# Weighted sums first, scores between them, row sums of four together: the dense attention steps of the later images

## The chip, the core and the metric

The kernel runs on one core of a Trainium2 chip. The metric is the device time of one execution in microseconds. Below, TensorE is the matrix engine (PE in the profile), VectorE is DVE, ScalarE is ACT, GpSimd is POOL, and SyncE (SP) issues most of the transfers.

## The reference

Two layers run one after the other on 8 images of 512 channels and 32 x 32 = 1024 tokens. Layer 0 is a group norm, attention with 8 heads whose q, k and v are rounded to 8 bits, a projection and a residual. Layer 1 is a group norm, attention with one head over all 512 channels, a projection and a residual. Cut to what matters here:

```python
# layer 0, x is (8, 512, 32, 32), T = 1024, 8 heads of 64 channels
h = group_norm(xf, gn_w, gn_b)
q, k, v = split(qkv_w @ h + qkv_b)          # each through fake_quant (8 bits)
w = softmax((q * scale)^T (k * scale))      # per head, T x T
a = einsum('bts,bcs->bct', w, v)            # weighted sums over the keys
x = xf + proj_w @ a + proj_b
# layer 1 on the result: one head of 512 channels
x = x + wp @ (softmax(q1 k1^T / sqrt(512)) v1) + bp
```

## The kernel before

**The phases.** First all images' q, k and v of layer 0 are computed and kept in DRAM, since the rounding needs the extremes over all images. Then layer 0's attention runs through all images as one stream, and layer 0's projection and the whole of layer 1 of an image run beside the attention of the images after it. The attention is a generator, `attention()`; the projection and layer 1 are another, `others()`. At each yield of `others()` the loop at the end (L1898 to L1900) lets the attention go one step further, and so attention steps come between the blocks of projection and layer 1 on TensorE, in the order written.

**Units.** A unit is one block of 128 keys, for a pair of heads and 512 queries: 8 images x 4 pairs x 2 halves x 8 blocks = 512 units. A step of the generator handles four of them, u to u+3. For a unit:

- `scores(u)` (L1009) makes the products of k and q: four matmuls for two units, "st<-q,k" in the profile, 64 rows for each head. They go to a tile of `pair_ps`, from the pool `ps_s`, which has two buffers; one tile takes two banks. ScalarE takes the exponential of the tile ("pt<-st,esc", L1034) and so frees it.
- `split(u)` (L1040) makes the f16 pair: the exponential cast to f16 (by ScalarE, or by GpSimd for every fourth unit) and the remainder, which VectorE computes ("two<-pt,two").
- `over_keys(us)` (L1090) makes the weighted sums, "av<-two,v": eight matmuls a unit, on 32 columns each.
- `totals(us)` (L1115) makes the row sums of the exponentials, "sm<-two,ones": four matmuls a unit, on 32 columns each.

A step works on weighted sums and row sums of u to u+3, on scores of u+6 to u+9, and on splits of u+6 to u+9.

**Three kinds of steps.** `dense` and `late` are set from what `others()` yields (L1899). A plain step (yield 1) takes the weighted sums and the row sums of four units together. A dense step (yield -1) takes two and two. A late step (yield 2) comes after the second half of the projection. Dense steps come just before a projection and between its two halves, `first()` at L1724 and `project` at L1292; image 0 has them at other places (the first step under the planner, between the halves of its projection, and in `layer1` at L1623).

**The projection.** `project` (L1260) makes, for each half, four output blocks of four matmuls over the channels ("pj<-ao,wp", two records each in the profile, 128 columns of 512). VectorE adds bias and residual to each block ("h<-pj,vec,h", L1278), which frees its bank. For image 0 the banks come from `ps_o`. For the later images `first()` passes `score_bank`, so the blocks take turns with the scores in the two buffers of `ps_s`:

```python
def score_bank(name):
    return pair_ps(name)[:, 0, :]
...
yield -1
yield from project(b + 1, score_bank)
yield 2
```

**What sets the order.** Every engine's instructions are recorded in program order and kept in it (`InOrder`, and `mm` at L208 for TensorE). Once `InOrder.planned` is set (L1893), small works of VectorE and ScalarE are held in lists with a cost and a due time, and are put into the stream by a model of the time: `pe.t` counts TensorE's, `do` and `fill` (L104, L127) place the works that fit before the next fixed one, and `awaits` moves `pe.t` for what a matmul waits for. The model's `scores` waits for the exponential that frees its tile; the projection's matmuls don't count that wait.

The function that the diff touches, and what calls it:

Of the kernel before, what the change touches and what calls it, by code (L numbers as in the profile page):

```python
# [58 lines left out]
def attn_pair_kernel(  # L59
# [12 lines left out]
    class InOrder:  # L72
# [74 lines left out]
        def settle(self, what):  # L147

            while True:
                i = next((i for i, c in enumerate(self.chores) if c[0] == what), None)  # L150
                if i is None:
                    return
                self.begin(i)
# [10 lines left out]
    def awaits(t):  # L164

        pe.t = max(pe.t, t + 0.1)
# [41 lines left out]
    def mm(ps, lhsT, rhs, **kw):  # L208
        ins = nc.tensor.matmul(ps, lhsT=lhsT, rhs=rhs, **kw).ins  # L209
        part = lhsT.shape[-1] / P if lhsT.shape[-1] in (32, 64) else 1.0  # L210
        if rhs.dtype in (BF, F16, F32R):
            part *= 0.25 * lhsT.shape[0] / P
        pe.t += math.prod(rhs.shape[1:]) * 1.677e-3 * part
        if last_mm[0] is not None:
            tc.add_manual_dep(ins, last_mm[0].name, IN_ORDER, reason="order")
        last_mm[0] = ins
# [90 lines left out]
    with ExitStack() as fast:  # L307
# [4 lines left out]
        def av_bank(name):  # L312
            return ps_v.tile([P, 512], F32, tag="v", name=name)
# [78 lines left out]
        with tc.tile_pool(name="p1w", bufs=1) as p1w, tc.tile_pool(  # L392
# [3 lines left out]
            def one(name):  # L396
                return ps_1.tile([P, 512], F32, tag="b", name=name)
# [313 lines left out]
            late = [one(f"qkps_0_{PAIRS}_{hf}") for hf in range(NH)]  # L711
# [201 lines left out]
        def plain(b, s):  # L913
            return b == 0 and s % 4 == 3
# [80 lines left out]
        def attention():  # L995
# [86 lines left out]
            def need(u):  # L1082

                if u in put_off:
                    put_off.pop(u)()
                while u not in ready:
                    e, name = (act, "cast") if u not in at_hand else (dve, "sum")
                    e.begin(next(i for i, c in enumerate(e.chores) if c[0] == name))

            def over_keys(us):  # L1090
                need(us[-1])
                awaits(ready[us[-1]])
                pe.t += 0.12
                for u in us:
                    b, j, hf, s = units[u]
                    if s == 0:
                        avs[b, j, hf] = av_bank(f"av_{b}_{j}_{hf}")
                    if plain(b, s):
                        for i in range(4):
                            r = slice(i * QUAD, (i + 1) * QUAD)  # L1100
                            mm(
                                avs[b, j, hf][r, :], lhsT=vfs[j][:, s // 4, r],
                                rhs=parts[u][:, i // 2, :], start=False, stop=(s == NT - 1),
                            )
                        continue
                    for w in range(2):
                        for i in range(4):
                            r = slice(i * QUAD, (i + 1) * QUAD)
                            mm(
                                avs[b, j, hf][r, :], lhsT=pairs[b, j][2][:, s, r],  # L1110
                                rhs=parts[u][:, w, i // 2, :], start=(s == 0 and w == 0),
                                stop=(s == NT - 1 and w == 1),
                            )

            def totals(us):  # L1115
                pe.t += 0.12
                for u in us:
                    b, j, hf, s = units[u]
                    if s == 0:
                        sms[b, j, hf] = av_bank(f"sm_{b}_{j}_{hf}")  # L1120
                    if plain(b, s) and s < NT - 1:
                        continue
                    for n in range(4):
                        row = sms[b, j, hf][n * QUAD : (n + 1) * QUAD, :]
                        if plain(b, s):
                            mm(row, lhsT=ones[:, 0:QUAD], rhs=parts[u - 4 + n // 2 * 4][:, n % 2, :],
                               start=False, stop=True)
                        else:
                            mm(row, lhsT=ones16, rhs=parts[u][:, n // 2, n % 2, :], start=(s == 0),
                               stop=(s == NT - 1))  # L1130
                    for v in (u - 4, u) if plain(b, s) else (u,):
                        del parts[v]
# [56 lines left out]
            for u in range(0, len(units), 4):  # L1189
                b, j, hf, s = units[u]  # L1190
                if hf == 0 and s == 0:
                    n = b * PAIRS + j + 1
                    if n < B * PAIRS:
                        pairs[divmod(n, PAIRS)] = load_pair(*divmod(n, PAIRS), u)
                    settle("qv")

                def two(what, v):  # L1200
                    if v < len(units):
                        what(v)
                        what(v + 1)

                pe.t += 0.12
                if not late:
                    two(scores, u + 6)
                if late:
                    over_keys((u, u + 1))
                    two(scores, u + 6)  # L1210
                    totals((u, u + 1))
                    over_keys((u + 2, u + 3))
                    totals((u + 2, u + 3))
                    two(split, u + 6)
                    two(scores, u + 8)
                elif dense:
                    over_keys((u, u + 1))
                    totals((u, u + 1))
                    two(split, u + 6)
                    two(scores, u + 8)  # L1220
                    over_keys((u + 2, u + 3))
                    totals((u + 2, u + 3))
                else:
                    over_keys(range(u, u + 4))
                    totals(range(u, u + 4))
                    two(split, u + 6)
                    two(scores, u + 8)
                if s == NT - 4:
                    finish(b, j, hf, u)
                two(split, u + 8)  # L1230
                pe.t += 0.15
                last = (j, hf, s) == (PAIRS - 1, NH - 1, NT - 4)
                yield b + last
# [616 lines left out]


        att = attention()
        done = 0
        dense = True
        late = False
# [42 lines left out]
        for n in others():  # L1898
            dense, late = n < 0, n == 2  # L1899
# [365 lines left out]
```

## Time and profile before

| what | value |
|---|---|
| time, median of 3 runs | 2581.56 us (2579.74 to 2581.93) |
| the profiled execution, its own time | 2581.92 us |
| its span | 2580.1 us |
| TensorE matmul busy | 2525.0 us, 98% of the span |
| VectorE busy | 1897.2 us, 74% |
| ScalarE busy | 1346.8 us, 52% |
| granted TensorE clock, mean | 0.995 |

The profile is one execution. A line of the profile's timeline has start, length, engine, source line, operation, what is written and read, shape, count, and in brackets the idle time ahead of it with what ended it. The matmuls' ends are modelled and overlap with the next, so the length of a block of matmuls is read from its start to the next block's. Since all engines' operations are recorded by helpers (L91, L209), operations are told apart by the tiles that they write and read.

### The profile page before, as it was taken

How to read it: one execution, taken by the hardware profiler on the slowest of the kernel's cores; microseconds unless marked ns; L12 is line 12 of the kernel's file. 1: busy time of each engine (PE TensorE's matmuls, PEld its weight loads, DVE VectorE, ACT ScalarE, POOL GpSimd, SP SyncE). 2: the span in 40 equal slices, each digit the busy share in tenths (PEclk: the TensorE clock that was granted, in tenths of full speed). 3: DMA queues.
4: the chain of work that ended last, by engine and by line, in shares of the span. 5: the costliest groups of instructions: out<-in, count | busy, mean ns of one | idle time of the engine just before them, and what ended most of it. 6: DMA issues, size and time to landing. Idle time of an engine off the chain costs nothing.

```text
span 2580.1 us, 38716 instructions
## 1 busy us (share of the span) xinstructions
PE 2525.0 (98%) x15670; PEld 1751.9 (68%) x15670; DVE 1897.2 (74%) x2747; ACT 1346.8 (52%) x1684; POOL 185.3 (7%) x167
## 2 busy tenths in 40 slices
PE   7999999998999999999999999999999999999998
PEld 4788888872247766775777577657756775777787
DVE  6788777667978777776777787777778777775544
ACT  3222222217947665665666466747665665664121
POOL 0000000001110001000100010010001000100000
PEclk9999999999999999999999999999999999999999
DMA  4343333336621232123213321332232123212211
GB/s 168 134 147 138 113 120 120 131 123 180 148 88 63 87 103 100 50 79 119 87 55 103 100 87 58 100 114 67 71 115 91 49 76 123 88 49 83 86 38 39
DMA packets 160189, 250.69 MB, mean 97 GB/s; under 512 B 27008, under 2 KB 93568, under 8 KB 158464
## 3 DMA queue, kind: packets, MB, share of 16 engines
q1 hardware_dynamic: 125264, 182.81, 21.3%
q10 hardware_dynamic: 30560, 57.71, 6.5%
q0 software_dynamic: 4176, 7.60, 1.6%
q8 instruction: 125, 2.05, 0.3%
q14 instruction: 64, 0.52, 0.1%
HBM read 153.64 MB, written 86.28 MB: 93 GB/s over the span
## 4 chain that ended last, share of the span: by engine, by line
PE 85%; DVE 5%; issue 2%; ACT 2%; DMA 1%; POOL 0%; SPq 0%; ACTq 0%; DVEq 0%; POOLq 0%
PE s L209 15%; PE o L209 13%; PE qkps L209 12%; PE pj L209 9%; PE av L209 8%; PE v2ps L209 7%; PE vps L209 6%; PE g L209 6%; PE st L209 4%; PE sm L209 3%; DVE two L91 2%; ACT pt L91 1%; DVE h L91 1%; PE fold L209 1%; DMA two<-spare 1%
## 5 line engine op out<-in xcount | busy, mean ns | idle before, releaser
L91 ACT ACTIVATE pt<-st,esc 128x1024 f32<-128x1024 f32 x467 | 496.4, 1114 | 333.8 <-PE st L209 316.3
L91 DVE TENSOR_TENSOR two<-pt,two 128x1024 f16<-128x1024 f32 x467 | 561.9, 1217 | 136.8 <-POOL two L1069 101.9
L91 ACT CAST two<-pt 128x1024 f16<-128x1024 f32 x346 | 350.7, 1055 | 7.7 <-ACT p L91 5.1
L209 PE MATMUL av<-two,v 128*32 128x512 f16 x3968 | 248.4, 383 | 8.2 <-DVE two L91 5.6
L1069 POOL CAST two<-pt 128x1024 f16<-128x1024 f32 x112 | 145.4, 1298 | 1412.2 <-ACT pt L91 714.8
L209 PE MATMUL s<-g,h 128*128 128x256 f32 x1024 | 233.4, 381 | 0.0
L209 PE MATMUL pj<-ao,wp 128*128 128x512 f32 x512 | 223.6, 595 | 0.0
L209 PEld LDWEIGHTS s<-g,h 128*128 128x128 f32 x1024 | 193.1, 190 | 30.8 <-issue 4.3
L91 ACT ACTIVATE u_ring<-qkps,qkbt 128x512 f32<-128x512 f32 x89 | 61.0, 685 | 252.5 <-PE qkps L209 235.7
L209 PEld LDWEIGHTS <-v 128*32 128x32 f16 x3968 | 92.3, 96 | 147.7 <-issue 75.2
L209 PE MATMUL s<-g,sums 128*128 128x256 f32 x768 | 178.5, 381 | 0.2 <-DVE p L91 0.2
L209 PEld LDWEIGHTS pj<-ao,wp 128*128 128x128 f32 x512 | 96.2, 190 | 121.2 <-issue 111.6
L209 PE MATMUL st<-q,k 64*128 64x512 bf16 x1024 | 164.4, 384 | 12.7 <-ACT pt L91 7.1
L209 PE MATMUL o<-p,v 128*128 128x256 f32 x768 | 175.2, 382 | 1.0 <-DVE p L91 1.0
L209 PEld LDWEIGHTS o<-p,v 128*128 128x128 f32 x768 | 144.4, 190 | 26.9 <-issue 5.7
L209 PEld LDWEIGHTS s<-g,sums 128*128 128x128 f32 x768 | 144.8, 190 | 24.3 <-issue 4.6
L209 PE MATMUL sm<-two,ones 128*32 128x512 f16 x1984 | 137.4, 382 | 0.0
L209 PE MATMUL qkps<-half,w_high 128*128 128x512 f32 x480 | 134.4, 403 | 0.0
L209 PE MATMUL qkps<-half,w_low 128*128 128x512 f32 x480 | 131.8, 397 | 2.3 <-DVE half L91 2.3
L209 PEld LDWEIGHTS <-k 64*128 64x128 bf16 x1024 | 35.0, 94 | 144.9 <-issue 142.8
L209 PE MATMUL qkps<-half,w_mix 128*128 128x512 f32 x480 | 131.2, 396 | 1.1 <-DVE half L91 1.1
L209 PE MATMUL v2ps<-wm,h 128*128 128x256 f32 x512 | 119.9, 384 | 1.9 <-ACT g L91 1.3
(225 smaller groups left out, 3906.5 us busy)
## 6 DMA issues: line engine op xcount, KB each, us to landing
rs<-rs_d SPq DMA_DIRECT2D x76, 256.0 KB
x<-in_x_dram SPq DMA_DIRECT2D x32, 512.0 KB
q_d<-wa SPq DMA_DIRECT2D x32, 512.0 KB
k_d<-wa SPq DMA_DIRECT2D x32, 512.0 KB
v_d<-v_ring SPq DMA_DIRECT2D x32, 512.0 KB
raw<-q_d SPq DMA_DIRECT2D x32, 512.0 KB
raw<-k_d SPq DMA_DIRECT2D x32, 512.0 KB
x_d<-h SPq DMA_DIRECT2D x64, 256.0 KB
```

Of the source, the lines that this page charges most:

```text
L91: ins = self.latest = op(*args, **kw).ins
L209: ins = nc.tensor.matmul(ps, lhsT=lhsT, rhs=rhs, **kw).ins
L1069: copy(two[:, 0], pt)
```

## The change

In dense steps under the planner, the scores of u+6 and u+7 no longer open the step: the weighted sums of u and u+1 do, then come those scores, then the weighted sums of u+2 and u+3, then the row sums of all four units, and the scores of u+8 and u+9 end the step. The dense steps of the first image's attention, which run before the planner is on, keep their order, as do plain and late steps.

```diff
                 pe.t += 0.12
-                if not late:
+                if not late and not (dense and InOrder.planned):
                     two(scores, u + 6)
                 if late:
                     over_keys((u, u + 1))
...
                     two(split, u + 6)
                     two(scores, u + 8)
+                elif dense and InOrder.planned:
+                    over_keys((u, u + 1))
+                    two(scores, u + 6)
+                    over_keys((u + 2, u + 3))
+                    totals(range(u, u + 4))
+                    two(split, u + 6)
+                    two(scores, u + 8)
                 elif dense:
                     over_keys((u, u + 1))
                     totals((u, u + 1))
                     two(split, u + 6)
                     two(scores, u + 8)
                     over_keys((u + 2, u + 3))
                     totals((u + 2, u + 3))
```

## The prediction

> **What bounds the kernel now.** I read the page first: busy shares, the chain, the costliest groups. Then the waits of TensorE alone, then the timeline of TensorE around one projection, because the change only moves matmuls there.
>
> ```profile
> PE 2525.0 (98%) x15670; PEld 1751.9 (68%) x15670; DVE 1897.2 (74%) x2747; ACT 1346.8 (52%) x1684; POOL 185.3 (7%) x167
> ...
> PE 85%; DVE 5%; issue 2%; ACT 2%; DMA 1%; POOL 0%; SPq 0%; ACTq 0%; DVEq 0%; POOLq 0%
> ```
>
> TensorE is busy 98% of the span and 85% of the chain that ended last. Past the first image it hardly waits: in all the waits of TensorE, "st" for the exponential (ACT pt) is 7.1 us in 15 pieces and "st" for the projection's eviction (DVE h) 3.1 us in 6. So a change to the order gains only what TensorE waits inside the changed steps, and costs whatever new wait it makes. One projection of a later image, TensorE's timeline (start, length shown, operation, count, idle before it and who ended it):
>
> ```profile
> 948.77 0.61 PE L209 MATMUL st<-q,k 64*128 64x512 bf16 x4
> 949.31 1.05 PE L209 MATMUL av<-two,v 128*32 128x512 f16 x16
> 950.18 0.60 PE L209 MATMUL sm<-two,ones 128*32 128x512 f16 x8
> 950.72 0.39 PE L209 MATMUL st<-q,k 64*128 64x512 bf16 x2
> 951.53 0.39 PE L209 MATMUL st<-q,k 64*128 64x512 bf16 x2 [0.42 <-ACT pt L91]
> 951.86 1.05 PE L209 MATMUL av<-two,v 128*32 128x512 f16 x16
> 952.73 0.60 PE L209 MATMUL sm<-two,ones 128*32 128x512 f16 x8
> 953.26 14.00 PE L209 MATMUL pj<-ao,wp 128*128 128x512 f32 x32
> 967.20 0.39 PE L209 MATMUL st<-q,k 64*128 64x512 bf16 x2
> 968.11 0.39 PE L209 MATMUL st<-q,k 64*128 64x512 bf16 x2 [0.52 <-DVE h L91]
> 968.43 1.05 PE L209 MATMUL av<-two,v 128*32 128x512 f16 x16
> 969.30 0.60 PE L209 MATMUL sm<-two,ones 128*32 128x512 f16 x8
> ```
>
> Ends overlap, so a block's length is taken from start to next start. The first dense step (before the projection) lasts 953.26 - 948.77 = 4.49 us with a hole of 0.6 at its second pair of scores, waiting for an exponential; the second (between the halves) 971.78 - 967.20 = 4.58 with a hole of 0.69, waiting for the last eviction of the half. The other five images that still have attention left beside their projection show the same two lengths within 0.02 us. Without holes both are 0.54 + 0.87 + 0.54 + 0.54 + 0.87 + 0.54 = 3.90.
>
> **What the Trainium skill says.** (1) "TensorEngine Tiling (Array Packing)", Key Properties: changing the tiling mode drains TensorE. Here scores use 64 rows, the weighted sums and row sums 32 columns, the projection the whole array. The trace agrees, at about 0.1 us a switch: 16 "av" before "sm" take 0.87, before "st" 0.98 (985.72 to 986.70); 8 "sm" before "av" 0.44, before "st" or "pj" 0.54. The number of switches stays five a step. (2) "ScalarE: Activation LUTs", What ACT_TABLE_LOAD costs: with one pointer operand 280 ns and 0.833 ns an element, and neighbours overlap by about 93 ns. For 1024 elements that is an estimate of 1.13 us; the page's row has 1114 ns, and four in a row took 4.14, so one each 1.01. (3) "Perfetto Trace Analysis", Optimization Strategy: the same gap repeating can mean that there isn't enough PSUM for the next tile. That is both holes here: scores, and from image 1 on the projection too, take turns on the two buffers of `ps_s`.
>
> **The change part by part.** No instruction is added or removed; 15 dense steps that have units left are reordered: two for each of images 1 to 6, and three around image 0's projection. Image 7's find no units left. The built program's order shows TensorE otherwise unchanged.
>
> *Row sums of four together.* Old: st, av, sm, st, av, sm. New: av 0.98, st 0.54, av 0.87, sm 0.97 (16 before "st": 935.92 to 936.89), st 0.54, sum 3.90. So the order itself is worth nothing.
>
> *Weighted sums first: what it covers.* In the step between halves the last eviction ends 0.86 us after the step begins; 0.98 us of av now lies before the scores, and that hole goes (-0.69). The units' f16 parts must be there 0.54 earlier for the first two, and at 1.52 instead of 3.1 for the next. DVE wrote all four before 948.39 in the first step, and during the 14 us projection in the second: no cost.
>
> *Scores between: what it covers.* With T the step's start: the first scores are at T+0.98, their exponentials start 0.43 later (967.20 to 967.63), at T+1.41 and 2.42, and end by T+3.53. The second scores come at 0.98 + 0.54 + 0.87 + 0.97 = T+3.36, their second pair at about T+3.57: no hole is left (-0.6).
>
> *Scores last: what it uncovers.* The first projection matmul needs the buffer of the third scores, so it waits for that exponential. Before, 1.41 us of av and sm lay between them. Now nothing does: scores at T+3.36, exponential 0.43 later, 1.11 long, and 0.05 from its end to the matmul (951.48 to 951.53): T+4.95. The step becomes 4.95 instead of 4.49 and of 4.58: +0.46 and +0.37. The second block needs the fourth exponential, done near T+5.9, and is reached at T+8.4. Behind the waiting matmul TensorE's whole queue stands: the projection, the scores after it, everything. Six images: 6 x 0.83 = **+5.0**.
>
> *Image 0, where the projection has its own pool.* The first of its steps runs 706.44 to 716.31, held by DVE twice: av waits until 709.65, and until 715.55 for the last unit. Scores and row sums filled part of those waits; now av waits first (709.65, done 710.61), scores to 711.15, av waits again to 715.55, then 0.22 + 0.97 + 0.54, end 717.28: +0.97. [...] The second step, 4.33, becomes 3.90: -0.43. The third (752.76 to 757.15, 4.39) is followed by a fold matmul in a score buffer: 4.95, +0.56. Together +1.10.
>
> *What moves behind.* DVE puts one split after an eviction instead of before, in the slack of the projection: nothing. SP's queue fetches v ahead of the reciprocals' broadcast, so an output scaling starts after an eviction; TensorE doesn't read it: nothing, unless that cover goes, then up to 0.8 (the wait "DVE kept_u <- DMA rs" there). In image 0 the planner orders some casts anew; one of 1.04 moves behind the eviction of g, for which TensorE now waits:
>
> ```profile
> 782.35 1.99 PE L209 MATMUL v2ps<-wm,h 128*128 128x256 f32 x8 [1.32 <-ACT g L91]
> ```
>
> I take -0.8 for it, bounds -1.3 (that wait gone) and +1.0 (a cast in the way elsewhere). Sum: +5.0 + 1.1 - 0.8 = **+5.3 us**. The profiled execution took 2581.92 (span 2580.1 and 1.8 around it), 0.36 above the median of the runs, 2581.56. So 2587.2 for the profile and **2586.9** for the median.
>
> **The rivals.** *A: the exponential is not in the way (faster).* If the first projection matmul found another buffer free, every step would be 3.90: 6 x (0.59 + 0.68) = 7.6 saved, image 0 -0.8 and +0.97 - 0.43 - 0.49; about 2581.56 - 8.4 = 2573. For it: the holes it closes are real and repeat. Against: score and projection blocks draw on one pool of two, four score tiles come directly before, and the sequence puts the first block on the third's buffer. It decides once the wait is under 0.6 us a step (4.95 then falls to the old 4.5); that would need an exponential ready about 0.4 us sooner. *B: partly covered (no difference).* If latencies are 0.1 shorter than I added, or image 0's replanning gains its full 1.3, the sum is +3 to +5, some 2585.5: for it, four of my terms are single readings. *C: the new order costs more.* If the planner, which doesn't count this wait, leaves DVE or ScalarE late in each image by another 0.2 to 0.4, +7 to +8, 2589. Against: TensorE stands still there, so the others gain time.
>
> **How the numbers follow.** 0.2% or 5.2 us is about what a measurement of this kernel can tell from no change; my sum lies on that edge. The sum with its own spread (+3.6 to +7.3) has 0.66, of which 0.42 above the edge: it reaches further up than down, since the covers named above can only be lost. B has 0.14, C 0.12, A 0.08. Slower by over 0.2%: 0.42 + 0.12 = 0.54; within: 0.24 + 0.14 = 0.38; faster: 0.08. Range: from 2582.5 to 2590.0, which takes in the sum's spread, B and most of C, and leaves out A.
>
> **What would show it.** In the profile after: TensorE's waits should have a new row, the projection waiting for ACT pt, about 0.9 to 1.05 us twelve times, some 12 us; "st" waiting for DVE h should vanish, "st" for ACT pt nearly so in these steps; dense steps should last 4.95 from start to start. Projection starting 0.54 after the scores proves A. A longer image period than 0.83 us more proves C.

## The result, and the profile after

The changed kernel took 2587.38 us in the median of 12 runs (2585.06 to 2592.04), the kernel before 2581.74 beside it (12 runs): a ratio of 1.0021, 95% interval 1.0013 to 1.0029. It is slower by 5.6 us between the medians, and by 3.4 to 7.5 us (0.13 to 0.29%) by the interval. The prediction was +5.3 us and 2586.9.

From the page of the profile after, the busy shares:

```profile
PE 2524.6 (98%) x15670; PEld 1748.9 (68%) x15670; DVE 1895.9 (73%) x2747; ACT 1349.3 (52%) x1684; POOL 188.5 (7%) x167
```

TensorE has the same instructions and the same busy time as before (2525.0), in a span that grew from 2580.1 to 2584.3. So nothing that it does became dearer in the sum; it stands still longer. Where, TensorE's waits tell (who waited for whom, us in total, times, the longest). Three rows of before:

```profile
PE st L209 <- ACT pt L91: 7.1, 15, 0.8
PE av L209 <- DVE two L91: 5.6, 7, 1.7
PE st L209 <- DVE h L91: 3.1, 6, 0.5
```

And of after:

```profile
PE pj L209 <- ACT pt L91: 11.8, 12, 1.0
PE av L209 <- DVE two L91: 8.3, 7, 3.3
...
PE st L209 <- ACT pt L91: 4.3, 8, 0.8
```

The first row is new: the projection waits for an exponential, 12 times, 0.98 us each. The row of "st" waiting for DVE h is gone, and "st" for ACT pt fell from 7.1 us to 4.3. The weighted sums' wait for DVE two grew by 2.7 us; that is image 0's first step, as the runs below show. The same stretch as the one shown of before, TensorE's timeline of after:

```profile
948.01 1.05 PE L209 MATMUL av<-two,v 128*32 128x512 f16 x16
948.99 0.60 PE L209 MATMUL st<-q,k 64*128 64x512 bf16 x4
949.53 1.05 PE L209 MATMUL av<-two,v 128*32 128x512 f16 x16
950.40 1.04 PE L209 MATMUL sm<-two,ones 128*32 128x512 f16 x16
951.37 0.62 PE L209 MATMUL st<-q,k 64*128 64x512 bf16 x4
952.97 14.00 PE L209 MATMUL pj<-ao,wp 128*128 128x512 f32 x32 [0.98 <-ACT pt L91]
966.90 1.05 PE L209 MATMUL av<-two,v 128*32 128x512 f16 x16
...
971.86 14.00 PE L209 MATMUL pj<-ao,wp 128*128 128x512 f32 x32 [0.98 <-ACT pt L91]
```

Both steps last 4.96 us from start to start (948.01 to 952.97, 966.90 to 971.86), 0.47 and 0.38 more than before; all twelve last 4.95 or 4.96. The scores run without a hole in them, the weighted sums ahead cover the last eviction, and then the projection waits for ScalarE, which began that exponential only at 951.80 (ScalarE's timeline of after):

```profile
949.42 2.12 ACT L91 ACTIVATE pt<-st,esc 128x1024 f32<-128x1024 f32 x2 [0.71 <-PE st L209]
951.80 2.12 ACT L91 ACTIVATE pt<-st,esc 128x1024 f32<-128x1024 f32 x2 [0.26 <-PE st L209]
```

ScalarE waited for TensorE (0.26) before the pair that TensorE then waits for: neither engine is too slow, the dependence simply has no other work in it.

### The profile page after: what moved, and what is told of

Read it like the earlier page. It is cut to its first block, busy times and chain, and to the rows that moved or that the text cites. A ratio compares the mean times of both kernels' runs of the same rounds, so it can differ in the third digit from the quotient of the medians.

```text
span 2584.3 us, 38709 instructions
## 1 busy us (share of the span) xinstructions
PE 2524.6 (98%) x15670; PEld 1748.9 (68%) x15670; DVE 1895.9 (73%) x2747; ACT 1349.3 (52%) x1684; POOL 188.5 (7%) x167
## 4 chain that ended last, share of the span: by engine, by line
PE 85%; DVE 5%; ACT 2%; issue 2%; DMA 1%; POOL 0%; ACTq 0%; SPq 0%; DVEq 0%; POOLq 0%
PE s L209 15%; PE o L209 13%; PE qkps L209 12%; PE pj L209 8%; PE av L209 8%; PE v2ps L209 7%; PE g L209 6%; PE vps L209 6%; PE st L209 4%; PE sm L209 4%; DVE two L91 2%; ACT pt L91 1%; PE fold L209 1%; DMA two<-spare 1%; DVE h L91 1%
## 5 line engine op out<-in xcount | busy, mean ns | idle before, releaser
L209 PE MATMUL g<-h,wa 128*128 128x256 f32 x512 | 121.1, 384 | 0.1
```

## The experiments

Theory: the whole loss is the projection's first matmul, which waits for the third exponential, since blocks of the projection and of scores share two buffers and nothing stands between them any more. Rivals: the loss comes from the works placed anew around image 0; the wait is for something else than the exponential's end; any cover would do.

The five kinds of dense steps got a name and an order each. A, B and C are image 0's (the first under the planner, the one between the halves of its projection, the one in `layer1`); X stands ahead of a later projection, Y between its halves. S1 and S2 are the two pairs of scores (S2 with the split ahead of it), O1 and O2 the weighted sums, T1, T2 the row sums of two units, T4 of four. The kernel before is `S1 O1 T1 S2 O2 T2` everywhere, after is `O1 S1 O2 T4 S2`:

```diff
-                elif dense and InOrder.planned:
-                    over_keys((u, u + 1))
...
+                elif kind:
+                    for op in ORDER[kind].split():
+                        if op == "S1":
+                            two(scores, u + 6)
+                        elif op == "S2":
+                            two(split, u + 6)
+                            two(scores, u + 8)
+                        elif op == "T4":
+                            totals(range(u, u + 4))
+                        else:
+                            us = (u, u + 1) if op[1] == "1" else (u + 2, u + 3)
+                            (over_keys if op[0] == "O" else totals)(us)
```

Ratios are to the kernel before, run beside each on the same chip.

| kernel | median us | before us | ratio | 95% interval |
|---|---|---|---|---|
| new order in X and Y alone | 2587.20 | 2580.56 | 1.0028 | 1.0017 to 1.0040 |
| new order in A, B, C alone | 2582.22 | 2580.56 | 1.0001 | 0.9993 to 1.0009 |
| as after, third exponential of half the size | 2582.01 | 2580.56 | 1.0005 | 0.9997 to 1.0013 |
| row sums last, sums of four between the scores | 2578.43 | 2580.56 | 0.9990 | 0.9982 to 0.9997 |
| row sums last, sums in pairs | 2586.93 | 2581.01 | 1.0027 | 1.0015 to 1.0039 |
| the parts put together | 2576.85 | 2581.01 | 0.9985 | 0.9978 to 0.9992 |

### The later images alone

```diff
-A B C: O1 S1 O2 T4 S2
+A B C: S1 O1 T1 S2 O2 T2
 X Y:   O1 S1 O2 T4 S2
```

> The new order in the twelve dense steps of images 1 to 6 alone, image 0 keeps the old one. Theory (the first projection matmul waits for the exponential of the last scores): steps of 4.96 us instead of 4.49 and 4.58, so +0.47 and +0.38 six times, +5.1 us against before. Rival (the loss comes from the replanned work around image 0): +0 to +1.5 us, and the waits of the projection are paid back elsewhere in the image.

The ratio is 1.0028, or +7.2 us with an interval of 4.4 to 10.3, and takes in the 5.1. In the profile the twelve steps are 4.96 again, and the row of the waits is that of after:

```profile
PE pj L210 <- ACT pt L92: 11.8, 12, 1.0
```

From image 1's projection to image 7's (its first matmul) TensorE's timeline has 1435.9 us (953.44 to 2389.35), the profile of before 1431.9 (953.26 to 2385.11): +4.1, with one step ahead fewer in it, for which 0.38 + 5 x 0.85 = 4.6 was due. The missing 0.5 is a wait that only before has: at 1730.86 a matmul waits for DVE g (0.23), and from one image's first step to the next it takes 240.71 us there, 240.21 to 240.35 in the other four. The later images carry the loss.

### Image 0 alone

```diff
 A B C: O1 S1 O2 T4 S2
-X Y:   O1 S1 O2 T4 S2
+X Y:   S1 O1 T1 S2 O2 T2
```

> The new order in image 0's three dense steps alone, later images keep the old one. Theory: the prediction's terms give +0.3 us against before (+0.97, -0.43, +0.56, -0.8); the profile of after shows image 0 dearer, +2.5 from the step under the slower clock, so +0.3 to +2.5 us, and this and the run with the later images alone add up to the whole change. Rival (image 0 carries the loss): +4 to +5.5 us.

1.0001: no loss that can be told, and an interval (-1.8 to +2.3 us) that leaves no room for +4. The profiles of one execution each agree: spans of 2583.9 us with the later images alone and 2580.6 with image 0 alone, +3.8 and +0.5 on 2580.1, where the whole change has +4.2. In the waits of this run the projection is not among the rows at all, and both of "st" are back, at 6.8 and 3.1. The weighted sums' wait for DVE two is that of after, 8.3, so it belongs to image 0:

```profile
PE av L210 <- DVE two L92: 8.3, 7, 3.3
...
PE st L210 <- ACT pt L92: 6.8, 14, 0.8
...
PE st L210 <- DVE h L92: 3.1, 6, 0.5
```

### Half an exponential

The new order everywhere, and the third unit's exponential over half of the queries:

```diff
-            def scores(u):
+            def scores(u, wide=512):
...
+                if wide < 512:
+                    nc.gpsimd.memset(pt[:, :, wide:512], 1.0)
...
-                    1.12, lambda: act.activation(pt, st, AF.Exp, scale=esc),
+                    1.12, lambda: act.activation(
+                        pt[:, :, 0:wide], st[:, :, 0:wide], AF.Exp, scale=esc
+                    ),
...
-                            two(scores, u + 8)
+                            if kind in "XY" and u + 8 < len(units):
+                                scores(u + 8, 256)
+                                scores(u + 9)
+                            else:
+                                two(scores, u + 8)
```

> As after, but in the dense steps of images 1 to 6 the third unit's exponential covers 256 of 512 queries of each head; the rest of its tile is set to one by GpSimd, so half of that unit's exponentials is left out. Theory (the wait follows this exponential's length): it gets about 0.43 us shorter (1024 elements 1.114 us, 512 elements of another activation 0.685), the projection starts at 4.53 instead of 4.96 in all twelve steps, 5.2 us less than after, so about as before to +2.5. Rival (the wait is for something else, the mode switch or the weights): steps stay at 4.96 and the time is that of after, +5.6.

TensorE's timeline of this kernel, the step ahead of image 1's projection:

```profile
950.69 1.05 PE L210 MATMUL av<-two,v 128*32 128x512 f16 x16
...
953.08 1.04 PE L210 MATMUL sm<-two,ones 128*32 128x512 f16 x16
954.05 0.62 PE L210 MATMUL st<-q,k 64*128 64x512 bf16 x4
955.22 1.13 PE L210 MATMUL pj<-ao,wp 128*128 128x512 f32 x2 [0.55 <-ACT pt L92]
```

TensorE's order is the same to the instruction, the exponential 0.43 us shorter, the wait 0.55 or 0.56 instead of 0.98 and the step 4.53 instead of 4.96, in all twelve. The time falls back to 1.0005 of before. This is the wait's cause: it moves by as much as that one exponential does.

What is left of the wait could still be the switch from scores to projection or the load of the weights. Image 0's second step in the profile after speaks against that. It has the same order, and the projection behind it has banks of its own (`ps_o`):

```profile
733.65 0.62 PE L209 MATMUL st<-q,k 64*128 64x512 bf16 x4
734.19 14.00 PE L209 MATMUL pj<-ao,wp 128*128 128x512 f32 x32
```

There the projection starts 0.54 us after the scores, without a wait, though it follows the same scores and loads weights of the same shape. And in image 0's third step a fold matmul, of another mode than the projection but in a score buffer, waits 0.98 us as the projection does (last experiment). So the wait comes with the shared buffers. A run in which the later images' projection has banks of its own was not made.

### Row sums between the last scores and the projection

First with the weighted sums of all four units between the two pairs of scores:

```diff
-X Y: O1 S1 O2 T4 S2
+X Y: S1 O1 O2 S2 T4
```

> Dense steps of images 1 to 6: scores, weighted sums of four units, scores, row sums of four units, then the projection; image 0 as before. Theory (two buffers and ScalarE's pace decide): the 0.97 us of row sums cover the third exponential; the step ahead of the projection is 3.98 instead of 4.49, the one between its halves keeps its hole for the eviction and is about 4.65 instead of 4.58; together -0.44 six times, -2.6 us against before. Rival (only the order of blocks counts, holes go where the scores stand later): 3.90 in both, -7.6 us. Rival (row sums of four together cost): no gain.

Timeline of TensorE, the first step and the start of the second:

```profile
947.63 0.60 PE L210 MATMUL st<-q,k 64*128 64x512 bf16 x4
948.16 1.91 PE L210 MATMUL av<-two,v 128*32 128x512 f16 x32
950.01 0.78 PE L210 MATMUL st<-q,k 64*128 64x512 bf16 x4
950.71 1.05 PE L210 MATMUL sm<-two,ones 128*32 128x512 f16 x16
951.69 14.00 PE L210 MATMUL pj<-ao,wp 128*128 128x512 f32 x32
965.62 0.39 PE L210 MATMUL st<-q,k 64*128 64x512 bf16 x2
966.53 0.39 PE L210 MATMUL st<-q,k 64*128 64x512 bf16 x2 [0.52 <-DVE h L92]
```

4.06 ahead of the projection (3.98 expected; the second scores take 0.70 instead of 0.54, still a little held by the second exponential) and 4.68 between its halves (965.62 to 970.30), where the eviction holds the scores as before. That makes -0.43 + 0.10 = -0.33 an image, -2.0 us; the ratio of 0.9990 is -2.6 us (-4.6 to -0.8). The same five blocks in another order are faster than both kernels, so row sums of four together can't be what costs; what decides is what stands on either side of the scores.

Then with the new order's first half, and only the row sums moved behind the last scores:

```diff
-X Y: O1 S1 O2 T4 S2
+X Y: O1 S1 O2 S2 T4
```

> Dense steps of images 1 to 6: weighted sums of two, scores, weighted sums of two, scores, and the row sums of four last; image 0 as before. 0.97 us of row sums now lie between the last scores and the projection. Theory (two score buffers and one exponential each 1.01 us on ScalarE): bringing the second scores forward only moves the wait to them; their second pair waits for the second exponential until 3.58, the row sums end at 4.88, so steps of 4.88 instead of 4.96 in after, +4.1 us against before. Rival (any 0.97 us of cover behind the scores hides the exponential): 3.98, -6.7 us against before.

Timeline of TensorE, the step between the halves:

```profile
965.14 1.05 PE L210 MATMUL av<-two,v 128*32 128x512 f16 x16
966.12 0.61 PE L210 MATMUL st<-q,k 64*128 64x512 bf16 x4
966.66 1.05 PE L210 MATMUL av<-two,v 128*32 128x512 f16 x16
967.72 0.39 PE L210 MATMUL st<-q,k 64*128 64x512 bf16 x2
968.72 0.39 PE L210 MATMUL st<-q,k 64*128 64x512 bf16 x2 [0.61 <-ACT pt L92]
969.04 1.05 PE L210 MATMUL sm<-two,ones 128*32 128x512 f16 x16
970.02 1.56 PE L210 MATMUL pj<-ao,wp 128*128 128x512 f32 x3
```

The projection no longer waits for the exponential, the scores do, and the step is 4.88 as worked out: cover behind the scores is of no use when it is taken from between them. The time, +7.0 us (3.9 to 10.1), is above the +4.1, though the interval still takes that in, and the profile has a reason for more: this order also has a wait "pj" for DVE h, 2.7 us in 4 pieces, and in four of the six images the first half of the projection takes 14.4 to 15.3 us instead of 13.93, 3.8 in all. In VectorE's timeline a scaling that waits for its reciprocals stands ahead of the projection's first eviction:

```profile
955.75 0.69 DVE L92 TENSOR_TENSOR kept_u<-kept_u,rs 128x512 f32<-128x512 f32 x1 [1.68 <-DMA rs<-rs_d]
956.48 0.88 DVE L92 SCALAR_TENSOR_TENSOR x<-kept_u,ob,x 128x256 f32<-128x256 f32 x2
957.27 0.75 DVE L92 SCALAR_TENSOR_TENSOR h<-pj,vec,h 128x512 f32<-128x512 f32 x1
```

In the kernel after, the planner puts that scaling behind the eviction; here it doesn't, so the first eviction starts only 6.5 us after the first block's start (957.27 against 950.75), and the third block, which takes the same buffer, waits for it.

### The parts put together

```diff
-A B C: O1 S1 O2 T4 S2
-X Y:   O1 S1 O2 T4 S2
+A C: S1 O1 T1 S2 O2 T2
+B:   O1 S1 O2 T4 S2
+X:   S1 O1 O2 S2 T4
+Y:   Oa S1 Ob S2 T4        # Oa: unit u, Ob: units u+1 to u+3
```

> Put together from what the runs showed. Ahead of the projection: scores, weighted sums of four, scores, row sums of four (4.06 measured). Between its halves: weighted sums of one unit, scores, weighted sums of three, scores, row sums of four; the one unit covers most of the eviction. In image 0 the new order in the second step only. Theory: the step between the halves is 0.54 + 0.54 and a hole of 0.16, then 1.41, 0.54 and a hole of 0.27, then 0.98, so 4.44 instead of 4.58; with -0.43 ahead of the projection and -0.43 once in image 0 -3.9 us against before. Rival (one unit's sums first bring the exponentials too late again): 4.6 to 4.7 between the halves, -2.5 us.

```profile
965.97 0.61 PE L210 MATMUL av<-two,v 128*32 128x512 f16 x8
966.52 0.76 PE L210 MATMUL st<-q,k 64*128 64x512 bf16 x4
967.21 1.48 PE L210 MATMUL av<-two,v 128*32 128x512 f16 x24
968.62 0.90 PE L210 MATMUL st<-q,k 64*128 64x512 bf16 x4
969.44 1.05 PE L210 MATMUL sm<-two,ones 128*32 128x512 f16 x16
970.42 1.12 PE L210 MATMUL pj<-ao,wp 128*128 128x512 f32 x2
```

4.45 between the halves (4.44 expected), and 0.9985: 4.2 us between the medians faster than before (2576.85 against 2581.01; 2.1 to 5.7 us by the interval), and some 9 us below the kernel after by the two ratios. One unit's sums ahead cover most of the eviction; the second scores still wait a little for the exponentials (0.82 from their start to the row sums instead of 0.54, as expected).

### Image 0's third step alone

The new order in C, all else as before; one execution.

> The new order in image 0's third dense step alone. Theory: that step is 4.96 instead of 4.39 with a fold matmul waiting about 1 us for the exponential, and the wait of v2ps for ACT g (1.32 before) goes, since casts are placed anew behind this step, so from there to image 1's projection 0.3 to 0.8 us less than before. Rival: that wait goes only when the step between the halves of image 0's projection is changed too, and stays here.

The step is 4.96 from start to start, and in TensorE's timeline the fold matmul waits, and v2ps no longer does:

```profile
760.19 1.06 PE L210 MATMUL wt_f<-wn_v,spare 128*32 128x512 f32 x8 [0.98 <-ACT pt L92]
...
782.51 3.94 PE L210 MATMUL v2ps<-wm,h 128*128 128x256 f32 x16
```

From this fold matmul to image 1's first projection matmul it takes 195.18 us (760.19 to 955.37), before 196.11 (757.15 to 953.26): -0.93, a little more than the 0.3 to 0.8 expected. In the kernel after it takes 195.64 (757.33 to 952.97) with image 1's first step 0.47 longer in it, which is the same. So it is this step's replanning that frees the eviction of g, not the steps ahead of it. Its time, 2583.18 us in one execution, tells nothing beside the range of the runs.

## Why the prediction was right

**Row sums of four together: worth nothing by themselves.** Right. 3.90 without holes was counted; image 0's second step, which has nothing to wait for, took 3.90 in the profile after.

**Weighted sums first: covers the eviction.** Right: the hole of 0.69 is gone in all six images, and with it the row "st <- DVE h".

**Scores between: no hole inside.** Right: the first scores run through to the sums in 0.54, and no idle time stands between the two pairs of the second ones.

**Scores last: uncovers the exponential.** Right, at 4.96 against 4.95 and a wait of 0.98 against 0.9 to 1.05. That it is this exponential is shown by the half-size run, and that the shared buffers tie the projection to it by image 0's second step. The size of the six images: 6 x (0.47 + 0.38) = 5.1, predicted 5.0; run alone they took the whole loss.

**Image 0: +0.3 predicted.** Within what the runs can tell (+0.3, -1.8 to +2.3). The terms for the order hold, and a term for the clock is missing. The second step was counted -0.43 and took 3.90 or 3.91 instead of 4.33 in all four profiles that have the new order there. The third was counted +0.56 and -0.8 behind it, and is +0.57 and -0.93. The first was counted +0.97 from the waits for VectorE. From the last pair of scores ahead of it to the end of the projection half behind it, the profiles with the old order in it have 26.5 to 26.6 us (before and two others) or 28.3 to 28.4 (three others), and the three with the new order 29.2, 29.4 and 29.8. What lies on top of 26.5, or of 26.5 + 0.97, is 1.7 to 2.4 us, and the granted clock accounts for that (last section); so +0.97 fits too. Such a stretch of low clock lay behind the first step's last wait in all three profiles with the new order, and in three of six with the old one; whether the order makes it likelier would take more executions, and stays open.

**The sum.** The path and the sizes of the later images' steps are shown. That the whole came within 0.3 us of the medians is in part luck: the interval is 4 us wide, and the clock around image 0 adds between nothing and 2.4 us.

**The rivals.** A (faster, no wait) fell: there is a wait of 0.98 twelve times, and its point of decision, a wait under 0.6, was met only with half the exponential left out (0.55), where the time came back to that of before. B (partly covered) fell for the later images. C, a late VectorE or ScalarE, didn't happen in the kernel after. Its sign was an image period more than 0.83 us longer: over five periods, from image 1's first step to image 6's, it is 1206.16 us against 1201.71, 0.89 a period, so 0.06 above where C had 0.2 to 0.4. It did happen in one experiment, with just the mechanism that the prediction named as the cover that could go: the scaling that waits for its reciprocals.

## What to carry to other kernels

Before a block of matmuls is moved, ask not only what it will cover where it goes, but what it covered where it stood: here 1.41 us of sums hid the rest of an exponential between scores and a projection that takes the same buffer, and no instruction tells of that dependence but the pool's turn. With two buffers the consumer must fit twice, between the producers and behind the last one; the gain came from splitting the cover work between both places, not from the block order as such. When a change moves only order, compare unblocked lengths first (3.90 on both sides here): if they are equal, all of the effect is in the waits, and it can be worked out to a few hundredths from start-to-start times, as long as the granted clock stays the same.

## What the runs showed of the hardware

Around the start of the planned part TensorE waits for VectorE, and there its granted clock drops to half for a while. In narrow windows it is 0.50 or 1.00, with nothing steady between. The columns of the rows are stretch, length, busy time and count of each engine, then the granted clock, DMA share and GB/s; first of before:

```profile
710.00:713.40 3.40, 3.40 (x32) 0.83 (x24) 0.32 (x1) 1.58 (x2) 1.04 (x1) 0.50 0.87 207
713.40:730.20 16.80, 15.05 (x52) 6.34 (x44) 15.95 (x18) 4.44 (x6) 0.88 (x1) 1.00 0.23 79
```

of after:

```profile
707.00:717.20 10.20, 7.56 (x46) 2.23 (x43) 5.91 (x5) 5.12 (x5) 2.84 (x2) 0.50 0.26 61
717.20:730.20 13.00, 13.00 (x31) 5.51 (x29) 9.03 (x11) 3.01 (x5) 0.00 (x0) 1.00 0.23 73
```

and of the parts put together, which has the old order in image 0's first step:

```profile
714.80:718.20 3.40, 3.40 (x6) 1.34 (x5) 3.18 (x3) 2.69 (x4) 1.14 (x1) 0.50 0.00 0
718.40:729.90 11.50, 11.50 (x31) 4.79 (x32) 9.32 (x12) 0.00 (x0) 0.04 (x1) 1.00 0.34 114
```

Each stretch of half clock here lasts 3.4 us in eight of the nine profiles; in that of after it is one of 10.2, three times as long. What it costs depends on what it falls on. Before, it ends ahead of the last wait for VectorE, which lasts until 715.55 in any case, and the projection half behind takes 13.94 us (716.31 to 730.25). In the parts put together a second stretch lies inside the projection half, which takes 15.63 (714.25 to 729.88): 1.7 more, half of 3.4. In after, the last wait ends at 712.33 and half clock at 717.2, so an estimate from these two is (717.2 - 712.33) / 2 = 2.4 us; 16 row sums took 1.87 us there from start to start (0.97 in the later images) and 4 scores 0.97 (0.54).

What brings the second stretch isn't shown. It isn't the new order alone, since three kernels with the old one there have it. Nor does the last wait's length tell: with the old order it was 1.88, 1.88 and 1.94 us in these three, and 1.75, 1.76 and 2.06 in the three without. The twelve waits of 0.98 us in the later images left no such trace: the projection halves behind them took 13.93, as before.
